# More of the softmax sums on GpSimd, and a new timetable for the side work, in a graph network with masked attention

## The chip, the cores and the metric

The kernel runs on one core of a Trainium2 chip. A core has five engines, each with an instruction stream of its own: TensorE (PE in the profile; PEld is its loading of weights), VectorE (DVE), ScalarE (ACT), GpSimd (POOL) and SyncE (SP), which issues most transfers. The metric is the device time of one execution, in microseconds (us); the time of a kernel is the median of several executions.

## The reference, cut to what matters

The input `x` is 8 batches of 2048 nodes with 256 features; `adj` is a 2048 x 2048 matrix of weights, with zeros. All is in float32. Layer 0 is a graph convolution with two batch norms, layer 1 an attention with 4 heads of 64 over the same nodes, masked where `adj` is 0. Each layer is added to its input, and a layer norm follows.

```python
# layer 0 (inner part cut): agg = A_hat @ x; h = relu(bn(agg @ W1.T)); out = bn(h @ W2.T)
x = _layernorm(x + _L0_gnn_ref(x, adj, ...), axis=-1)

# layer 1
qkv = h @ W                                    # h is the x of the line above
q, k, v = ...                                  # 4 heads of 64
mask = jnp.where(adj == 0, -jnp.inf, 0.0)
scores = jnp.einsum('bhid,bhjd->bhij', q, k) / np.sqrt(HEAD_DIM) + mask
attn = jax.nn.softmax(scores, axis=-1)
out = jnp.einsum('bhij,bhjd->bhid', attn, v)
x = _layernorm(x + out, axis=-1)
```

## The kernel before

The first part (layer 0) is not touched by the change. The attention works in **units**. A unit is one batch `b`, one pair of heads `hp` (2 pairs) and one chunk `c` of 512 query nodes (4 chunks), so a batch has 8 units and the kernel 64. A unit has 16 **steps**, one for each tile of 128 key nodes. In a step TensorE computes the scores of the tile that lies three steps ahead (`scores`), VectorE masks them from PSUM into a tile `prob`, ScalarE takes the exponential in place, and TensorE multiplies the tile of this step with `v` into the PSUM tile `out_ps` (`weigh`). The maximum of a row is not subtracted; the sums are tested at the end, and another path (`attention_with_maxima`) runs if one is out of range.

The divisor of the softmax is a sum over all key nodes. GpSimd adds the `prob` tiles of a unit one onto another (`acc`), and TensorE sums over the partitions by a multiplication with ones. The last tiles of a unit do not go through GpSimd: TensorE takes them directly.

```python
PE_SUM = 3

def add_up(g):
    u, j = divmod(g, NT)                       # NT = 16
    if j == 1:
        accs[u] = ap_.tile([P, 2, CH], F32, name="acc")
        nc.gpsimd.tensor_add(accs[u], probs[g - 1], probs[g])          # L454
    elif 1 < j < NT - PE_SUM:
        nc.gpsimd.tensor_add(accs[u], accs[u], probs[g])               # L456

def finish_out(u):
    ots[u] = ap_.tile([P, CH], F32, name="ot")
    nc.scalar.copy(ots[u], outs[u][:, 0, :])                           # L460
    nc.vector.tensor_add(ots[u], outs.pop(u)[:, 1, :], ots[u])         # L461

def finish_sums(u):
    pm = ps_m.tile([P, BR], F32, name="pm")
    parts = [probs.pop(g) for g in range((u + 1) * NT - PE_SUM, (u + 1) * NT)]
    parts.append(accs.pop(u))
    for n, part in enumerate(parts):
        for h in range(2):
            for q in range(2):
                ... nc.tensor.matmul(pm[r0 : r0 + 32, :], ones[:, :32], part[...], ...)   # L472
    ...
    sts[u] = ap_.tile([P, BR], F32, name="sm")
    nc.scalar.copy(sts[u], pm)                                         # L480

# finish_turn_sums (L486): sums transposed, reciprocals; finish_turn (L499): output transposed;
# finish (L507): output times reciprocal, added to the chunk x1 (VectorE)
```

Beside this the units carry side work: the input of the next batch is made chunk by chunk (load of `y` and `x`; second batch norm `bn` on ScalarE; `norm`: transposes by TensorE, addition and statistics on VectorE; `root`: four small GpSimd instructions, L91, L93, L272, L273, among them a power of -0.5; `apply`: the rescaling on ScalarE, L277; `turn`: transposes back, L332, and a copy, L338; `project`: q, k and v, L363 and L375). A finished chunk gets its last layer norm (`emit_stats`, `root`, `emit`). All small results of TensorE share the PSUM tile name `pm`, which has two buffers; `out_ps` has one, `prob` has 13. A table tells at which step which side task stands:

```python
for u in range(NU - 1):
    b, hp, c = units[u]
    at_step(u + 1, 0, finish_sums, u)
    at_step(u + 1, 3, finish_turn_sums, u)
    at_step(u + 1, 3, finish_turn, u)
    at_step(u + 1, 3, finish, u, 0)
    at_step(u + 1, 4, finish, u, 1)
    if hp == HP - 1:
        j = 6 if c == 2 else 12
        at_step(u + 1, j, inp.emit_stats, b, c)
        at_step(u + 1, j + 2, inp.root, b, c)
        for half in range(2):
            at_step(u + 1, j + 5 + half, inp.emit, b, c, half)
...
# projections stand at steps 6, 9, 12 of a unit; a chunk of the next batch takes two units

with tc.manual_schedule(engines=IN_ORDER):     # TensorE, VectorE, ScalarE, GpSimd: as written
    for g in range(LEAD):                      # LEAD = 3
        mask_scores(g, scores(g))
        exps(g)
    for g in range(NU * NT):
        u, j = divmod(g, NT)
        ahead = g + LEAD < NU * NT
        if ahead:
            st = scores(g + LEAD)              # L415
        if j == NT - 1:
            weigh(g)                           # L445
            finish_out(u)
        if ahead:
            mask_scores(g + LEAD, st)          # L427
            exps(g + LEAD)                     # L433
        for f, args in side.get((u, j), ()):
            f(*args)
        if j < NT - 1:
            weigh(g)
        add_up(g)
```

Of the kernel before, what the change touches and what calls it, by code (L numbers as in the profile page):

```python
# [8 lines left out]
F32 = mybir.dt.float32  # L9
U8 = mybir.dt.uint8  # L10
AF = mybir.ActivationFunctionType
# [15 lines left out]
def tile_gcn_then_masked_attention(  # L27
# [15 lines left out]
    nc = tc.nc  # L43
    PSUM = bass.MemoryType.PSUM
    P = 128
    B, N, D = x.shape
# [3 lines left out]
    NT = N // P  # L50
    ND = D // P
    NH = H // P
    NO = O // P
    CH = 512
    NCH = N // CH
# [226 lines left out]
    class Layer1Input:  # L282
# [4 lines left out]
            self.pool, self.psum, self.x1_bufs = pool, psum, x1_bufs  # L287
            self.x1, self.x1t, self.yt, self.qkv, self.ln = {}, {}, {}, {}, {}

        def load(self, b, c):  # L290
            if c == 0:
                self.x1t[b] = self.pool.tile([P, ND, N], F32, name="x1t", bufs=1)
            y = self.yt[b, c] = self.pool.tile([P, NO, CH], F32, name="yt", bufs=1)
            nc.sync.dma_start(y, y_d[b * NCH + c])
            t = self.x1[b, c] = self.pool.tile([P, TPC, D], F32, name="x1", bufs=self.x1_bufs)
            nc.sync.dma_start(t, rows(b, c, x))

        def bn(self, b, c):
            y = self.yt[b, c]
            for o in range(NO):  # L300
                nc.scalar.activation(
                    y[:, o, :], y[:, o, :], AF.Identity,
                    bias=sh2[:, o : o + 1], scale=sc2[:, o : o + 1],
                )

        def norm(self, b, c, half):
            y = self.yt[b, c]
# [18 lines left out]

        def turn(self, b, c, half):
            t = self.x1[b, c]
            pm = self.psum.tile([P, ND, BR], F32, name="pm")
            for d in range(ND):  # L330
                for i in range(IT):
                    nc.tensor.transpose(  # L332
                        pm[:, d, i * P : (i + 1) * P],
                        t[:, IT * half + i, d * P : (d + 1) * P],
                        ident,
                    )
            r0 = c * CH + half * BR
            nc.scalar.copy(self.x1t[b][:, :, r0 : r0 + BR], pm)  # L338

        def emit_stats(self, b, c):  # L340
            ln = self.ln[b, c] = LayerNorm(self.pool, self.x1[b, c])
            ln.stats(range(TPC))

        def emit(self, b, c, half):
            self.apply(b, c, half)
# [46 lines left out]
    def attention():  # L392


        with tc.tile_pool(name="attn", bufs=2) as ap_, tc.tile_pool(
# [5 lines left out]
            units = [(b, hp, c) for b in range(B) for hp in range(HP) for c in range(NCH)]  # L401
            probs, accs, outs, ots, sts, pms = {}, {}, {}, {}, {}, {}

            PE_SUM = 3

            def scores(g):
                u, j = divmod(g, NT)
# [42 lines left out]
            def add_up(g):  # L450
                u, j = divmod(g, NT)
                if j == 1:
                    accs[u] = ap_.tile([P, 2, CH], F32, name="acc")
                    nc.gpsimd.tensor_add(accs[u], probs[g - 1], probs[g])  # L454
                elif 1 < j < NT - PE_SUM:
                    nc.gpsimd.tensor_add(accs[u], accs[u], probs[g])  # L456

            def finish_out(u):
# [4 lines left out]
            def finish_sums(u):  # L463

                pm = ps_m.tile([P, BR], F32, name="pm")
                parts = [probs.pop(g) for g in range((u + 1) * NT - PE_SUM, (u + 1) * NT)]
                parts.append(accs.pop(u))
                for n, part in enumerate(parts):
                    for h in range(2):
                        for q in range(2):  # L470
                            r0 = 32 * (2 * h + q)
                            nc.tensor.matmul(  # L472
                                pm[r0 : r0 + 32, :], ones[:, :32],
                                part[:, h, q * BR : (q + 1) * BR],
                                start=(n == 0), stop=(n == len(parts) - 1),
                            )
                for g in range(u * NT, (u + 1) * NT - PE_SUM):
                    del probs[g]
                sts[u] = ap_.tile([P, BR], F32, name="sm")
                nc.scalar.copy(sts[u], pm)  # L480
# [30 lines left out]

            LEAD = 3
            side = {}

            def at_step(u, j, f, *args):
                u, j = u + j // NT, j % NT
                side.setdefault((u, j), []).append((f, args))

            per_b = HP * NCH
            for u in range(NU - 1):
                b, hp, c = units[u]
                at_step(u + 1, 0, finish_sums, u)
                at_step(u + 1, 3, finish_turn_sums, u)
                at_step(u + 1, 3, finish_turn, u)
                at_step(u + 1, 3, finish, u, 0)
                at_step(u + 1, 4, finish, u, 1)
                if hp == HP - 1:
                    j = 6 if c == 2 else 12  # L530
                    at_step(u + 1, j, inp.emit_stats, b, c)
                    at_step(u + 1, j + 2, inp.root, b, c)
                    for half in range(2):
                        at_step(u + 1, j + 5 + half, inp.emit, b, c, half)
            for b in range(B):
                u0 = b * per_b
                for c in range(NCH):

                    for n, w in enumerate((1, 2, 0)):
                        at_step(u0 + c, (6, 9, 12)[n], inp.project, b, 1, c, w)  # L540
                    if b + 1 == B:
                        continue

                    late = 3 * (c == NCH - 1)
                    u = u0 + 3 + c
                    at_step(u - 1, 15 + late, inp.load, b + 1, c)
                    at_step(u, 2 + late, inp.bn, b + 1, c)
                    for half in range(2):
                        at_step(u, 6 + 3 * half + late, inp.norm, b + 1, c, half)
                    at_step(u, 11 + late, inp.root, b + 1, c)  # L550
                    for half in range(2):
                        at_step(u, 13 + half + (4 if late else 0), inp.apply, b + 1, c, half)
                    for half in range(2):
                        at_step(u + 1, 4 if late else 1, inp.turn, b + 1, c, half)
                    for n, w in enumerate((1, 2, 0)):
                        at_step(u + 1, (8, 10, 13)[n] if late else (6, 9, 12)[n],
                                inp.project, b + 1, 0, c, w)

            for c in range(NCH):
                inp.load(0, c)  # L560
                inp.bn(0, c)
                for half in range(2):
                    inp.norm(0, c, half)
                inp.root(0, c)
                for half in range(2):
                    inp.apply(0, c, half)
                for half in range(2):
                    inp.turn(0, c, half)
                for w in range(3):
                    inp.project(0, 0, c, w)  # L570

            with tc.manual_schedule(engines=IN_ORDER):
                for g in range(LEAD):
# [10 lines that stand above are left out]
                    if ahead:  # L584
                        mask_scores(g + LEAD, st)
                        exps(g + LEAD)
                    for f, args in side.get((u, j), ()):
                        f(*args)
                    if j < NT - 1:
                        weigh(g)  # L590
                    add_up(g)
                u = NU - 1
                b, _, c = units[u]
                finish_sums(u)
                finish_turn_sums(u)
                finish_turn(u)
                for half in range(2):
                    finish(u, half)
                inp.emit_stats(b, c)
                inp.root(b, c)  # L600
                for half in range(2):
                    inp.emit(b, c, half)

    def attention_with_maxima():

        with tc.tile_pool(name="full", bufs=2) as ap_, tc.tile_pool(
# [8 lines left out]
            inp = Layer1Input(ap_, ps_m, NCH)  # L615
            for b in range(B):
                for c in range(NCH):
                    inp.load(b, c)
                    inp.bn(b, c)
                    for half in range(2):  # L620
                        inp.norm(b, c, half)
                    inp.root(b, c)
                    for half in range(2):
                        inp.apply(b, c, half)
                    for half in range(2):
                        inp.turn(b, c, half)
# [41 lines left out]
                                z, po, sm, z, op0=ALU.mult, op1=ALU.add  # L668
                            )
                for c in range(NCH):  # L670
                    inp.emit_stats(b, c)
                    inp.root(b, c)
                    for half in range(2):
                        inp.emit(b, c, half)
# [66 lines left out]
```

## Time and profile before

| | |
|---|---|
| time, median of 3 | 4022.19 us (4021.13 to 4022.88) |
| profiled execution | span 4024.4 us |
| masking, VectorE, L427 | 1024 times 1219 ns |
| exponential, ScalarE, L433 | 1024 times 1056 ns |
| addition of a `prob` tile, GpSimd, L456 | 704 times 2365 ns |
| sums of `prob` tiles on TensorE, L472 | 96.2 us in all |
| sums of `acc` on TensorE, L472 | 39.4 us in all |

The profile is that of one execution. Busy time is the time in which an engine had at least one instruction in work; shares are of the whole span, in which layer 0 takes the first 1500 us and the attention the rest. In timelines a line gives the start and the duration in us, then engine, source line, operation, the tiles written and read, and how many like instructions were put together ("x8"); a bracket names the idle time before and what ended it. A float32 product appears as two matmul records. TensorE's ends are modelled, so differences between starts are the better measure.

### The profile page before, as it was taken

What the parts mean: (1) busy time and instruction counts of PE and PEld (TensorE: products, weight loads), DVE (VectorE), ACT (ScalarE), POOL (GpSimd) and SP (SyncE); (2) the same over time, 40 slices, a digit from 0 to 9 for tenths busy, and PEclk for the clock granted to TensorE, in tenths of its full rate; (3) what the DMA queues carried; (4) which work ended last, traced back from release to release, by engine and by line L of the source; (5) the groups of instructions that cost most, each with busy time, mean ns of one, the idle gap of its engine ahead of it and who ended that gap; (6) DMA issues with size and microseconds to landing.
All of it is one profiled execution on the core that took longest, in us unless ns stands there. A gap on an engine that the chain in (4) does not pass through costs nothing.

```text
span 4024.4 us, 57339 instructions
## 1 busy us (share of the span) xinstructions
PE 3814.2 (95%) x24226; PEld 1580.8 (39%) x24226; DVE 1938.5 (48%) x2874; ACT 1634.9 (41%) x2005; POOL 1965.4 (49%) x1103
## 2 busy tenths in 40 slices
PE   3599999999997998999999999999999999999997
PEld 3244444444443443333333333333333333333332
DVE  6411111111112443666666666666666666666665
ACT  6000000000001434555555556556555555555554
POOL 0000000000000003778778777777787877877887
PEclk7799999999998998999999999999999999999998
DMA  5110110111003761001001001001001001000000
GB/s 209 65 53 29 45 52 34 50 53 52 32 31 131 233 205 64 5 13 38 12 17 38 12 17 38 12 17 38 12 12 43 12 12 43 12 12 24 10 1 23
DMA packets 77229, 181.80 MB, mean 45 GB/s; under 512 B 6176, under 2 KB 55840, under 8 KB 66592
## 3 DMA queue, kind: packets, MB, share of 16 engines
q1 hardware_dynamic: 67600, 123.49, 9.3%
q0 software_dynamic: 9360, 54.53, 3.3%
q8 instruction: 192, 3.15, 0.3%
q14 instruction: 77, 0.63, 0.1%
HBM read 106.70 MB, written 71.30 MB: 44 GB/s over the span
## 4 chain that ended last, share of the span: by engine, by line
PE 86%; ACT 4%; DVE 3%; issue 1%; POOL 1%; DMA 1%; SPq 0%; ACTq 0%; DVEq 0%; POOLq 0%
PE pa L183 22%; PE out_ps L445 20%; PE st L415 19%; PE pm L363 6%; PE py L229 6%; PE ph L195 5%; PE pm L375 3%; ACT prob L433 2%; ACT x L277 2%; PE pm L472 2%; DVE prob L427 2%; POOL acc L456 1%; PE pm L312 1%; PE pm L499 1%; PE pm L332 1%
## 5 line engine op out<-in xcount | busy, mean ns | idle before, releaser
L456 POOL TENSOR_TENSOR acc<-acc,prob 128x1024 f32<-128x1024 f32 x704 | 1664.9, 2365 | 168.5 <-ACT prob L433 120.6
L427 DVE SCALAR_TENSOR_TENSOR prob<-mask,st 128x1024 f32<-128x1024 uint8 x1024 | 1241.8, 1219 | 648.6 <-PE st L415 640.3
L433 ACT ACTIVATE prob<-prob 128x1024 f32<-128x1024 f32 x1024 | 1080.5, 1056 | 1049.1 <-DVE prob L427 1041.3
L445 PE MATMUL out_ps<-prob,v 64*64 64x512 f32 x8192 | 1089.1, 598 | 0.1
L415 PE MATMUL st<-qt,kt 64*64 64x512 f32 x8192 | 1074.3, 590 | 0.9 <-DVE prob L427 0.9
L183 PE MATMUL pa<-at,xb 128*128 128x512 f32 x2048 | 886.1, 593 | 47.0 <-DMA xb<-in_x_dram 47.0
L183 PEld LDWEIGHTS pa<-at,xb 128*128 128x128 f32 x2048 | 389.8, 190 | 537.7 <-issue 537.7
L204 POOL DMA_DIRECT2D h_d<-h x32 | 17.3, 540 | 1151.3 <-ACT h L202 1151.3
L415 PEld LDWEIGHTS st<-qt,kt 64*64 64x64 f32 x8192 | 313.4, 133 | 567.5 <-issue 505.3
L202 ACT ACTIVATE h<-ph,b1s 128x512 f32<-128x512 f32 x128 | 87.9, 687 | 1066.0 <-PE ph L195 1066.0
L445 PEld LDWEIGHTS out_ps<-prob,v 64*64 64x64 f32 x8192 | 281.6, 132 | 508.7 <-issue 438.7
L190 DVE COPY ag<-pa 128x512 f32<-128x512 f32 x64 | 44.2, 691 | 823.7 <-PE pa L183 823.7
L454 POOL TENSOR_TENSOR acc<-prob 128x1024 f32<-128x1024 f32 x64 | 152.0, 2375 | 284.1 <-ACT prob L433 284.1
L363 PE MATMUL pm<-x1t,wq 128*128 128x512 f32 x512 | 254.8, 622 | 0.9 <-ACT x1t L338 0.9
L229 PE MATMUL py<-hin,w2s 128*128 128x512 f32 x512 | 222.6, 598 | 21.4 <-ACT hin L222 21.4
L195 PE MATMUL ph<-ag,w1s 128*128 128x512 f32 x512 | 231.1, 599 | 0.0
L203 DVE BATCH_NORM_STATS2 st<-h 128x6 f32<-128x512 f32 x128 | 88.9, 694 | 157.1 <-ACT h L202 157.1
L229 PEld LDWEIGHTS py<-hin,w2s 128*128 128x128 f32 x512 | 98.1, 192 | 145.8 <-issue 114.0
L363 PEld LDWEIGHTS pm<-x1t,wq 128*128 128x128 f32 x512 | 88.1, 191 | 160.3 <-issue 150.9
L222 ACT ACTIVATE hin<-hin,sh,sc 128x512 f32<-128x512 f32 x128 | 93.4, 801 | 138.1 <-DMA hin<-h_d 138.1
L195 PEld LDWEIGHTS ph<-ag,w1s 128*128 128x128 f32 x512 | 94.6, 190 | 131.3 <-issue 107.2
L277 ACT ACTIVATE x<-x,ln_nm,ln_rs 128x256 f32<-128x256 f32 x256 | 136.1, 585 | 24.2 <-POOL ln_nm L273 24.2
(83 smaller groups left out, 1815.3 us busy)
## 6 DMA issues: line engine op xcount, KB each, us to landing
h_d<-h POOLq DMA_DIRECT2D x32, 1024.0 KB, 4.1
hin<-h_d SPq DMA_DIRECT2D x32, 1024.0 KB, 5.9
a<-in_adj_dram SPq DMA_DIRECT2D x16, 1024.0 KB, 7.1
xb<-in_x_dram SPq DMA_DIRECT2D x8, 2048.0 KB, 8.1
y_d<-y POOLq DMA_DIRECT2D x32, 512.0 KB, 6.1
yt<-y_d SPq DMA_DIRECT2D x32, 512.0 KB, 3.2
x<-in_x_dram SPq DMA_DIRECT2D x32, 512.0 KB, 3.9
out_dram<-x SPq DMA_DIRECT2D x32, 512.0 KB, 2.9
```

The costliest lines, as they stand in the source:

```text
L183: nc.tensor.matmul(pa, xb[:, m, d * P : (d + 1) * P], at[:, m, c * CH : (c + 1) * CH], start=(m == 0), stop=(m == NT - 1),)
L195: nc.tensor.matmul(ph, w1s[:, d, f * P : (f + 1) * P], ag[:, d, :], start=(d == 0), stop=(d == ND - 1),)
L229: nc.tensor.matmul(py, w2s[:, f, o * P : (o + 1) * P], h[:, f, :], start=(f == 0), stop=(f == NH - 1),)
L277: nc.scalar.activation(self.t[:, i, :], self.t[:, i, :], AF.Identity, bias=self.nm[:, i : i + 1], scale=self.rs[:, i : i + 1],)
L363: nc.tensor.matmul(pm, wq[:, d, wcols], xt[:, d, cols], start=(d == 0), stop=(d == ND - 1))
L375: nc.tensor.matmul(pm[:, j * P : (j + 1) * P], xt[:, d, t * P : (t + 1) * P], wq[:, d, wcols], start=(d == 0), stop=(d == ND - 1),)
L415: nc.tensor.matmul(st[r * HD : (r + 1) * HD, h, :], kt[hs, j * P + r * HD : j * P + (r + 1) * HD], qt[hs, cols], start=True, stop=True,)
L427: nc.vector.scalar_tensor_tensor(p, mask[:, j, cols][:, None, :].to_broadcast([P, 2, CH]), MASKED, st, op0=ALU.mult, op1=ALU.add,)
L433: nc.scalar.activation(probs[g], probs[g], AF.Exp)
L445: nc.tensor.matmul(outs[u][hs, r, :], inp.qkv[b, hp][2][rs, j, hs], probs[g][rs, h, :], start=(j == 0), stop=(j == NT - 1),)
L454: nc.gpsimd.tensor_add(accs[u], probs[g - 1], probs[g])
L456: nc.gpsimd.tensor_add(accs[u], accs[u], probs[g])
```

## The change

The change does three things. It gives GpSimd 15 of the 16 `prob` tiles of a unit (13 before) and TensorE one directly, except in the last three units, where TensorE takes four. It moves the sums of a unit from step 0 of the next unit to step 4, and lets each unit begin with a projection instead (steps 0, 6 and 10). And it draws out the making of a chunk over three units, so that statistics, roots and rescalings stand some steps apart, and the two halves of a transpose are not in the same step. The aim is to take work from TensorE and to have its program wait for no other engine. The rows of the table have numbers with fractions now, which only order the tasks within a step.

```diff
-            PE_SUM = 3
+            def on_pe(u):
+                return 4 if u >= NU - NCH + 1 else 1
...
-                elif 1 < j < NT - PE_SUM:
+                elif 1 < j < NT - on_pe(u):
...
-            for u in range(NU - 1):
+            for u in range(NU):
                 b, hp, c = units[u]
-                at_step(u + 1, 0, finish_sums, u)
-                at_step(u + 1, 3, finish_turn_sums, u)
-                at_step(u + 1, 3, finish_turn, u)
-                at_step(u + 1, 3, finish, u, 0)
-                at_step(u + 1, 4, finish, u, 1)
+                at_step(u + 1, 4, finish_sums, u)
+                at_step(u + 1, 6, finish_turn_sums, u)
+                at_step(u + 1, 6.2, finish_turn, u)
+                at_step(u + 1, 6.2, finish, u, 0)
+                at_step(u + 1, 7, finish, u, 1)
                 if hp == HP - 1:
-                    j = 6 if c == 2 else 12
-                    at_step(u + 1, j, inp.emit_stats, b, c)
-                    at_step(u + 1, j + 2, inp.root, b, c)
                     for half in range(2):
-                        at_step(u + 1, j + 5 + half, inp.emit, b, c, half)
+                        at_step(u + 1, 10.3 + 3 * half, inp.emit_stats, b, c, half)
+                        at_step(u + 2, 3 + half, inp.emit, b, c, half)
+                    at_step(u + 2, 2, inp.root, b, c)
+
+            PROJECT = (0.1, 6.1, 10.1)
+
+            def project_at(u, b, hp, c):
+                for w in range(3):
+                    at_step(u, PROJECT[w], inp.project, b, hp, c, w)
+
             for b in range(B):
                 u0 = b * per_b
+                project_at(u0, b, 0, NCH - 1)
                 for c in range(NCH):
-                    for n, w in enumerate((1, 2, 0)):
-                        at_step(u0 + c, (6, 9, 12)[n], inp.project, b, 1, c, w)
+                    project_at(u0 + 1 + c, b, 1, c)
                     if b + 1 == B:
                         continue
-                    late = 3 * (c == NCH - 1)
                     u = u0 + 3 + c
-                    at_step(u - 1, 15 + late, inp.load, b + 1, c)
-                    at_step(u, 2 + late, inp.bn, b + 1, c)
-                    for half in range(2):
-                        at_step(u, 6 + 3 * half + late, inp.norm, b + 1, c, half)
-                    at_step(u, 11 + late, inp.root, b + 1, c)
+                    at_step(u, 1, inp.load_y, b + 1, c)
+                    at_step(u, 5, inp.load_x, b + 1, c)
+                    for o in range(NO):
+                        at_step(u, 5 + o, inp.bn, b + 1, c, o)
+                    at_step(u, 10, inp.norm, b + 1, c, 0)
+                    at_step(u + 1, 0, inp.norm, b + 1, c, 1)
+                    at_step(u + 1, 4, inp.root, b + 1, c)
                     for half in range(2):
-                        at_step(u, 13 + half + (4 if late else 0), inp.apply, b + 1, c, half)
-                    for half in range(2):
-                        at_step(u + 1, 4 if late else 1, inp.turn, b + 1, c, half)
-                    for n, w in enumerate((1, 2, 0)):
-                        at_step(u + 1, (8, 10, 13)[n] if late else (6, 9, 12)[n],
-                                inp.project, b + 1, 0, c, w)
+                        at_step(u + 1, 7 + half, inp.apply, b + 1, c, half)
+                        at_step(u + 1, 10.2 + 3 * half, inp.turn, b + 1, c, half)
+                    if c < NCH - 1:
+                        project_at(u + 2, b + 1, 0, c)
...
-                for w in range(3):
+                for w in range(3 if c < NCH - 1 else 0):       # ahead of the loop, first batch
                     inp.project(0, 0, c, w)
```

What is left out here splits `load`, `bn` and `emit_stats` into the parts that the table names, and has the last units' side tasks run out after the loop (`for u in (NU, NU + 1)`) in place of a written tail.

More of the change, by code (lines that the diff above doesn't have):

```diff
@@ L288, in __init__, with load_y, load_x, bn @@
             self.x1, self.x1t, self.yt, self.qkv, self.ln = {}, {}, {}, {}, {}
-        def load(self, b, c):
-            if c == 0:
-                self.x1t[b] = self.pool.tile([P, ND, N], F32, name="x1t", bufs=1)
+        def load_y(self, b, c):
             y = self.yt[b, c] = self.pool.tile([P, NO, CH], F32, name="yt", bufs=1)
             nc.sync.dma_start(y, y_d[b * NCH + c])
+        def load_x(self, b, c):
             t = self.x1[b, c] = self.pool.tile([P, TPC, D], F32, name="x1", bufs=self.x1_bufs)
             nc.sync.dma_start(t, rows(b, c, x))
-        def bn(self, b, c):
+        def bn(self, b, c, o):
             y = self.yt[b, c]
[L300 to L304, printed above, removed]
+            nc.scalar.activation(
+                y[:, o, :], y[:, o, :], AF.Identity,
+                bias=sh2[:, o : o + 1], scale=sc2[:, o : o + 1],
+            )
         def norm(self, b, c, half):
@@ L328, in turn @@
             t = self.x1[b, c]
+            if b not in self.x1t:
+                self.x1t[b] = self.pool.tile([P, ND, N], F32, name="x1t", bufs=1)
             pm = self.psum.tile([P, ND, BR], F32, name="pm")
@@ L338, in turn, with emit_stats @@
             nc.scalar.copy(self.x1t[b][:, :, r0 : r0 + BR], pm)
-        def emit_stats(self, b, c):
-            ln = self.ln[b, c] = LayerNorm(self.pool, self.x1[b, c])
-            ln.stats(range(TPC))
+        def emit_stats(self, b, c, half):
+            if half == 0:
+                self.ln[b, c] = LayerNorm(self.pool, self.x1[b, c])
+            self.ln[b, c].stats(range(IT * half, IT * (half + 1)))
         def emit(self, b, c, half):
@@ L465, in finish_sums @@
                 pm = ps_m.tile([P, BR], F32, name="pm")
-                parts = [probs.pop(g) for g in range((u + 1) * NT - PE_SUM, (u + 1) * NT)]
+                parts = [probs.pop(g) for g in range((u + 1) * NT - on_pe(u), (u + 1) * NT)]
                 parts.append(accs.pop(u))
@@ L476, in finish_sums @@
                             )
-                for g in range(u * NT, (u + 1) * NT - PE_SUM):
+                for g in range(u * NT, (u + 1) * NT - on_pe(u)):
                     del probs[g]
@@ L517, in at_step @@
             def at_step(u, j, f, *args):
-                u, j = u + j // NT, j % NT
-                side.setdefault((u, j), []).append((f, args))
+                tasks = side.setdefault((u, int(j)), [])
+                tasks.append((j, f, args))
+                tasks.sort(key=lambda task: task[0])
             per_b = HP * NCH
-            for u in range(NU - 1):
+            for u in range(NU):
                 b, hp, c = units[u]
-                at_step(u + 1, 0, finish_sums, u)
-                at_step(u + 1, 3, finish_turn_sums, u)
-                at_step(u + 1, 3, finish_turn, u)
-                at_step(u + 1, 3, finish, u, 0)
-                at_step(u + 1, 4, finish, u, 1)
+                at_step(u + 1, 4, finish_sums, u)
[3 more added lines that the diff above has]
+                at_step(u + 1, 7, finish, u, 1)
@@ L559, in attention @@
+                    at_step(u, 10, inp.norm, b + 1, c, 0)
+                    at_step(u + 1, 0, inp.norm, b + 1, c, 1)
+                    at_step(u + 1, 4, inp.root, b + 1, c)
+                    for half in range(2):
+                        at_step(u + 1, 7 + half, inp.apply, b + 1, c, half)
+                        at_step(u + 1, 10.2 + 3 * half, inp.turn, b + 1, c, half)
+                    if c < NCH - 1:
+                        project_at(u + 2, b + 1, 0, c)
             for c in range(NCH):
-                inp.load(0, c)
@@ L561, in attention @@
-                inp.bn(0, c)
+                inp.load_y(0, c)
+                inp.load_x(0, c)
+                for o in range(NO):
+                    inp.bn(0, c, o)
                 for half in range(2):
@@ L586, in attention @@
                         exps(g + LEAD)
-                    for f, args in side.get((u, j), ()):
+                    for _, f, args in side.get((u, j), ()):
                         f(*args)
@@ L591, in attention @@
                     add_up(g)
[L592 to L602, printed above, removed]
+                for u in (NU, NU + 1):
+                    for j in range(NT):
+                        for _, f, args in side.get((u, j), ()):
+                            f(*args)
     def attention_with_maxima():
@@ L617, in attention_with_maxima @@
                 for c in range(NCH):
-                    inp.load(b, c)
-                    inp.bn(b, c)
+                    inp.load_y(b, c)
+                    inp.load_x(b, c)
+                    for o in range(NO):
+                        inp.bn(b, c, o)
                     for half in range(2):
@@ L670, in attention_with_maxima @@
                 for c in range(NCH):
-                    inp.emit_stats(b, c)
+                    for half in range(2):
+                        inp.emit_stats(b, c, half)
                     inp.root(b, c)
```

## The prediction

> **What bounds the kernel now.** I read the page's first part, then the busy time in one stretch, then the waits of TensorE there, then the timelines of TensorE and GpSimd over one unit. First the page, busy time by engine:
>
> ```profile
> PE 3814.2 (95%) x24226; PEld 1580.8 (39%) x24226; DVE 1938.5 (48%) x2874; ACT 1634.9 (41%) x2005; POOL 1965.4 (49%) x1103
> ```
>
> GpSimd's 49% hides that it works only in the attention, from about 1550 us on. So take the attention alone. A batch is 8 units of 16 steps, and it repeats every 307.09 us. Busy times in one such stretch (PE, PEld, DVE, ACT, POOL):
>
> ```profile
> 2022.25:2329.34 307.09, 303.00 (x2610) 118.99 (x2609) 199.38 (x296) 173.08 (x209) 240.55 (x129) 1.00 0.07 22
> ```
>
> TensorE is busy 303.00 of 307.09 at clock 1.00, GpSimd 240.55 (78%). What TensorE waits for in the other 4.1 us (us in total, times, longest):
>
> ```profile
> PE pm L332 <- ACT sm L480: 2.4, 3, 0.8
> PE pm L332 <- ACT prob L433: 1.7, 1, 1.7
> ```
>
> Both stand at the turning of a new chunk (L332): three times because the two pm buffers of PSUM are still held by the sums of the unit just ended, once because the rescaling came late. TensorE executes in program order, so **a microsecond taken out of its work is a microsecond of time**, as long as nobody else falls behind. One plain unit on TensorE (start, duration):
>
> ```profile
> 2226.21 1.04 PE L415 MATMUL st<-qt,kt 64*64 64x512 f32 x8
> 2227.18 1.50 PE L472 MATMUL pm<-prob,ones 128*32 128x256 f32 x24
> 2228.49 0.61 PE L472 MATMUL pm<-acc,ones 128*32 128x256 f32 x8
> 2229.04 1.09 PE L445 MATMUL out_ps<-prob,v 64*64 64x512 f32 x8
> 2229.95 1.04 PE L415 MATMUL st<-qt,kt 64*64 64x512 f32 x8
> ...
> 2233.38 1.04 PE L415 MATMUL st<-qt,kt 64*64 64x512 f32 x8
> 2234.35 0.44 PE L486 MATMUL pm<-ident,sm 128*128 128x128 f32 x2
> 2234.62 0.60 PE L499 MATMUL pm<-ident,ot 128*128 128x128 f32 x4
> 2235.16 1.09 PE L445 MATMUL out_ps<-prob,v 64*64 64x512 f32 x8
> 2236.06 1.04 PE L415 MATMUL st<-qt,kt 64*64 64x512 f32 x8
> ```
>
> Read the differences of starts. A bare step (scores and weighing) takes 1.717 us, 16 of them 27.47. The step with the sums takes 2229.95 - 2226.21 = 3.74, so the sums cost 2.02; three tiles of them cost 2228.49 - 2227.18 = 1.31, that is **0.44 us a tile**. The turning of sums and output (L486, L499) costs 2.68 - 1.72 = 0.96. Read in the same way, the three projections of a unit cost 2.07, 2.14 and 2.08. Together 36.74; the next unit's sums start 36.75 us later. The same unit on GpSimd, then a root:
>
> ```profile
> 2226.34 2.37 POOL L454 TENSOR_TENSOR acc<-prob 128x1024 f32<-128x1024 f32 x1 [3.06 <-ACT prob L433]
> 2230.12 26.80 POOL L456 TENSOR_TENSOR acc<-acc,prob 128x1024 f32<-128x1024 f32 x11 [1.41 <-ACT prob L433]
> 2263.09 2.37 POOL L454 TENSOR_TENSOR acc<-prob 128x1024 f32<-128x1024 f32 x1 [6.17 <-ACT prob L433]
> ...
> 2325.61 0.23 POOL L91 TENSOR_SCALAR ln_rs<-ln_mv 128x4 f32<-128x4 f32 x1
> ```
>
> An add comes every 26.80 / 11 = 2.436 us. The second add starts 3.78 us after the first, held by its tile. 6.17 us are free at the unit's end. The four instructions of a root run from 2325.61 to the next add at 2327.50: 1.89 us.
>
> **What the Trainium skill says.** "GPSIMD Engine Reference", section "Elementwise — side-by-side cycle accounting", gives 4497 ns for a two-input fp32 add of 2048 elements; half of it is an estimate of 2250 ns for our 1024. The trace has 2365 ns; I use the trace. The same page, "Specifications", says that GpSimd's SBUF interface is shared with VectorE and collides with VectorE instructions that have two SBUF inputs or run in a two-port mode. Our masking reads one input from PSUM, and the 572 adds of the middle batches take 2351/2365/2391 ns (min, median, max) beside a VectorE 65% busy: no collision shows. "TensorEngine Tiling (Array Packing)", "Key Properties", says that a change of tiling mode drains TensorE. The trace agrees: scores (64x64) to sums takes 0.97 instead of 0.86, weighing to scores after it 0.91, so each side group costs some 0.15 beyond its matmuls. "Perfetto Trace Analysis", "Optimization Strategy", says that the same gap repeating on the engine that should be saturated can mean too few buffers: the 0.8 us at L332, three times a batch, is that.
>
> **The change part by part.**
>
> *Sums.* For units 0 to 60 TensorE sums one tile and the accumulator, not three tiles and the accumulator: 2 x 0.44 = 0.88 us a unit less. Units 61 to 63 sum four tiles, 0.44 more each.
>
> *GpSimd.* Two more adds a unit, 14. A plain unit is 3.78 + 13 x 2.436 = 35.45 us from the first add to the end of the last. A root inside the run (step 4, in four units of a batch) adds 1.89; a root at step 2 lies between the first and the second add, where 1.41 us are idle anyway, and adds 0.5. Over a batch: 8 x 35.45 + 4 x 1.89 + 4 x 0.5 = 293.2.
>
> *Sums at step 4, a projection at step 0.* The projection (2.07) takes the place of the sums (2.02) as what TensorE does while ScalarE and VectorE empty the output PSUM (585 and 691 ns, L460, L461), so no wait opens there. The sums move four steps (about 9 us) later, so GpSimd's accumulator is not waited for even if it is a few us late.
>
> *Merged groups.* The turning goes into the step of the second projection: one side group less, about 0.1 us saved. Norm transposes were beside a projection and stay so; one turning of the new chunk is now beside a projection and the other stands alone, about the same sum as the pair before.
>
> *The 4.1 us.* The halves of the turning are now three steps apart, and the roots 2 to 4 steps ahead of the rescaling. Where three pm tiles follow one another in one step (steps 6 and 10), a projection of 2 us lies between the first and the third, longer than the copy that frees the first (VectorE: up to 1.22 of masking, then 0.17 or 0.69). I expect these waits gone.
>
> A plain unit is then 36.75 - 0.88 - 0.10 = 35.77 on TensorE; a batch 303.0 - 8 x 0.98 = **295.2**, against 293.2 on GpSimd. TensorE stays the bound, narrowly.
>
> *Start.* The last chunk's first projections (three, 5.4 us) leave the stretch ahead of the loop for unit 0, which gives its own to unit 1. Unit 0's weighing now waits until chunk 3 is turned (before: at 1579.7), then needs 0.9 + 15 x 1.72 + 2.07 + 2.14 + 1.9 = 32.8: unit 1 at 1612.5, against 1612.0 before. But steps of unit 0 no longer stand between the transposes of chunks 1 to 3, where they delayed the chain by 1 to 3 us each. I choose 1608.
>
> *Units 1 to 55.* 7 x 295.2 - 35.8 = 2030.6: unit 56 at 3638.6 (before 3725.3).
>
> *Last batch.* Five units with projections, 5 x 35.77 = 178.9; unit 61 without: 27.5 + 1.15 + 0.96 = 29.6; two with four tiles: 30.9 each; and these three have nothing at step 0 to cover the emptying of the output, about 0.85 us each, 2.6. Sum 272.9: 3911.5.
>
> *Tail.* Before, the last weighing ended at 3992.2 and the program at 4024.4, 32.2 us, with this wait in it:
>
> ```profile
> PE pm L472 <- POOL acc L456: 4.3, 1, 4.3
> ```
>
> The last units were paced by GpSimd (12 adds and a root, 31.1 us). With 11 adds (26.8) it is ahead, the wait goes, a tile of 0.44 comes: 28.4. End at 3939.9 in the profile's span. The profiled span is 2.2 us over the median of the times: **3938 us**.
>
> **The rivals.** (1) *GpSimd becomes the bound.* Its batch is 293 of 295. If adds took 0.1 us more when back to back, 13 x 8 x 0.1 = 10 us a batch, it would pace the kernel at 303, and the end would be near 3995. For it: the thin margin. Against: the adds already run eleven back to back at 2.436. (2) *A new PSUM wait takes the old one's place:* three pm tiles in one step, four to twelve times a batch. At 0.5 us each that is 2 to 6 us a batch, 3952 to 3980. For it: the waits of 0.8 now are of this kind. Against: the projection in between. (3) *A rescaling waits for a root behind a busy GpSimd,* ScalarE's exponentials wait behind it, then TensorE. For it: the 1.7 us now; against: at least one step, mostly three, between them. About 1 us a batch, 3945. (4) *The sums were hidden anyway, so nothing is gained.* 303.00 busy of 307.09 speaks against it.
>
> **Range and chances.** The start is uncertain by 4 us, the tail by 3, a leftover wait of 0 to 2 us a batch adds up to 14; below, merged groups could give 0.1 us a unit more. I take 3926 to 3960. Two per cent is at 3941.7, just above my value: faster by over 2% 0.55, within 2% 0.43, slower 0.02.
>
> **What would show it.** Batch period 295 us, TensorE busy at least 99% of it; the sums of probability tiles about 37 us instead of 96 in all; adds still 2.37 us, GpSimd some 290 us a batch; no waits at L332. It is wrong if waits at L332, L499 or L472 fill more than 2 us a batch, or if the adds grow.

## The result, and the profile after

The changed kernel takes 3921.4 us (3918.9 to 3922.8), against 4022.5 for the kernel before: a ratio of 0.9746, 95% interval 0.9729 to 0.9763. The gain of 101 us is larger than predicted (84), and the time lies 4.6 us below the stated range.

The page's first part, busy time by engine:

```profile
PE 3732.8 (95%) x23274; PEld 1553.8 (40%) x23274; DVE 1935.4 (49%) x2874; ACT 1641.3 (42%) x2005; POOL 2245.5 (57%) x1222
```

TensorE has 81 us less to do, GpSimd 280 us more, VectorE and ScalarE the same. A batch repeats every 292.13 us, 14.96 less than before. Busy times in one batch (PE, PEld, DVE, ACT, POOL, then clock and transfers):

```profile
2009.88:2302.01 292.13, 292.13 (x2488) 115.59 (x2484) 198.88 (x296) 173.94 (x208) 278.18 (x144) 1.00 0.07 23
```

TensorE is never idle in it. The 4.1 us of waits a batch are gone. In the whole attention after unit 0, up to the final test of the sums, the list of TensorE's waits has two entries, both in the last units (us in total, times, longest):

```profile
PE out_ps L449 <- DVE ot L465: 1.7, 3, 0.6
PE pm L490 <- ACT sm L484: 1.6, 1, 1.6
```

The timeline of TensorE over one unit shows where its work went (start, duration):

```profile
1982.77 1.04 PE L419 MATMUL st<-qt,kt 64*64 64x512 f32 x8
1983.74 0.64 PE L476 MATMUL pm<-prob,ones 128*32 128x256 f32 x8
1984.19 0.61 PE L476 MATMUL pm<-acc,ones 128*32 128x256 f32 x8
1984.74 1.09 PE L449 MATMUL out_ps<-prob,v 64*64 64x512 f32 x8
1985.65 1.04 PE L419 MATMUL st<-qt,kt 64*64 64x512 f32 x8
...
1987.36 1.04 PE L419 MATMUL st<-qt,kt 64*64 64x512 f32 x8
1988.33 0.44 PE L490 MATMUL pm<-ident,sm 128*128 128x128 f32 x2
1988.61 1.88 PE L365 MATMUL pm<-x1t,wq 128*128 128x512 f32 x4
1990.33 0.60 PE L503 MATMUL pm<-ident,ot 128*128 128x128 f32 x4
1990.86 1.09 PE L449 MATMUL out_ps<-prob,v 64*64 64x512 f32 x8
1991.77 1.04 PE L419 MATMUL st<-qt,kt 64*64 64x512 f32 x8
```

From scores to scores the step with the sums takes 2.88 us: 1.16 for the sums, where it was 2.02. The step in which the turning stands around a projection takes 1991.77 - 1987.36 = 4.41, so the group costs 2.69. Apart, before, the same matmuls cost 0.96 + 2.07 = 3.03. **Standing together saves 0.34 us**, and no instruction was dropped. Where it lies shows beside the projection that stands alone at step 0 of the same unit:

```profile
1974.79 1.98 PE L365 MATMUL pm<-x1t,wq 128*128 128x512 f32 x4
1976.71 1.09 PE L449 MATMUL out_ps<-prob,v 64*64 64x512 f32 x8
```

Start to start, the four products take 1.92 us up to the weighing, but 1.72 up to the transposes at step 6: 0.20 lies inside this block, and only about 0.15 at the edges of the group (0.97 and 0.91 where a bare step has 0.86). The new chunk's second turning, which stands alone, shows the same from the other side:

```profile
2078.85 1.04 PE L419 MATMUL st<-qt,kt 64*64 64x512 f32 x8
2079.82 0.66 PE L333 MATMUL pm<-ident,x 128*128 128x128 f32 x4
2080.41 1.09 PE L449 MATMUL out_ps<-prob,v 64*64 64x512 f32 x8
2081.32 1.04 PE L419 MATMUL st<-qt,kt 64*64 64x512 f32 x8
```

2.47 - 1.72 = 0.75 us for four transposes alone. The same four beside a projection add 0.43 (that step goes from 4.26 to 4.69).

GpSimd is now nearly full, too. Its waits in the same batch:

```profile
POOL acc L460 <- ACT prob L437: 3.5, 3, 1.4
POOL acc L458 <- ACT prob L437: 0.4, 1, 0.4
```

It waits only 3.9 us of 292.1; the other idle time, some 10 us, lies between its own instructions (an add takes 2.37 us, as before, and one starts every 2.436). VectorE now waits for GpSimd to free a `prob` tile, 6.0 us a batch; TensorE does not.

### The profile page after: what moved, and what is told of

It is laid out like the page before. It is cut to its first block, busy times and chain, and to the rows that moved or that the text cites. A ratio compares the mean times of both kernels' runs of the same rounds, so it can differ in the third digit from the quotient of the medians.

```text
span 3918.3 us, 55545 instructions
## 1 busy us (share of the span) xinstructions
PE 3732.8 (95%) x23274; PEld 1553.8 (40%) x23274; DVE 1935.4 (49%) x2874; ACT 1641.3 (42%) x2005; POOL 2245.5 (57%) x1222
## 4 chain that ended last, share of the span: by engine, by line
PE 93%; DVE 1%; POOL 1%; DMA 1%; ACT 1%; issue 0%; SPq 0%; POOLq 0%; DVEq 0%; ACTq 0%
PE out_ps L449 23%; PE pa L183 23%; PE st L419 22%; PE pm L365 6%; PE py L229 6%; PE ph L195 6%; PE pm L377 3%; PE pm L476 2%; PE pm L311 1%; PE pm L333 1%; PE pm L503 1%; PE pm L490 1%; DVE at L168 1%; POOL acc L460 1%; DMA hin<-h_d 0%; ACT x L277 0%
## 5 line engine op out<-in xcount | busy, mean ns | idle before, releaser
L460 POOL TENSOR_TENSOR acc<-acc,prob 128x1024 f32<-128x1024 f32 x823 | 1948.5, 2368 | 101.7 <-ACT prob L437 43.9
L449 PE MATMUL out_ps<-prob,v 64*64 64x512 f32 x8192 | 1077.0, 596 | 1.7 <-DVE ot L465 1.7
L229 PE MATMUL py<-hin,w2s 128*128 128x512 f32 x512 | 222.9, 598 | 21.6 <-ACT hin L222 21.6
L238 POOL DMA_DIRECT2D y_d<-y x32 | 17.1, 533 | 224.2 <-DVE y L236 224.2
```

The lines of the kernel that those rows point to most:

```text
L229: nc.tensor.matmul(py, w2s[:, f, o * P : (o + 1) * P], h[:, f, :], start=(f == 0), stop=(f == NH - 1),)
L449: nc.tensor.matmul(outs[u][hs, r, :], inp.qkv[b, hp][2][rs, j, hs], probs[g][rs, h, :], start=(j == 0), stop=(j == NT - 1),)
```

## The experiments

The theory (A): TensorE is the bound and runs in program order, so each microsecond of its work or its waits is one of time; the gain is tiles, waits and merged groups. The rivals: GpSimd paces the changed kernel (C); the sums were hidden and the timetable did it all (B); and about the size of a merged group, my own 0.10 us. Times are medians of four or more runs.

**The timetable alone.**

```diff
 def on_pe(u):
-    return 4 if u >= NU - NCH + 1 else 1
+    return 3
```

> The changed kernel with three prob tiles summed by TensorE in every unit, as before: the new timetable alone. Theory A (TensorE is the bound, and its work decides): 61 units get 2 tiles back at 0.44 us, three units lose one, +52.4 us against the changed kernel's 3921, so about 3974 (3970 to 3979); batch period 292.1 + 7.0 = 299.2 us, TensorE busy all of it, GpSimd at some 240 us a batch. So the timetable is worth about 48 us of the 101 and the tiles 53. Rival B (the sums were hidden and the timetable brought everything): about 3921. Rival C (GpSimd paces the changed kernel, so giving it less work brings something back): less than +40 us.

Measured: 3974.0 us, ratio to before 0.9882 (0.9866 to 0.9899). The batch is 299.03 us, TensorE busy all of it, GpSimd 240.28. With the new timetable in place two tiles a unit are worth 52.6 us; the timetable itself is worth 48.3. B and C fall: giving GpSimd less to do brought nothing back.

**The tiles alone**, in the kernel before:

```diff
-PE_SUM = 3
+PE_SUM = 1
```

> The kernel before with 15 prob tiles added on GpSimd in every unit (PE_SUM = 1), sums still at step 0: the tiles alone. Theory A: 0.88 us a unit less on TensorE, and the accumulator is ready just in time in most units (35.4 us of adds from step 0, sums at some 37 us), while the last four units, which have no projections, are paced by GpSimd at 36 us instead of 31: 4022 - 53 + 20 + a few us of waits for the accumulator, about 3992 (3980 to 4005). Rival (without the move to step 4 TensorE waits for the accumulator in every unit, 1 to 2 us): 4030 to 4090, and waits of the sums for GpSimd of 60 us or more. Rival (hidden sums): 4022 or more.

Measured: 4013.1 us, 0.9976 (0.9969 to 0.9983), slower than expected: without the new timetable only 9 of the 53 us arrive. What TensorE waits for the accumulator, in one batch of the middle and then in the last units:

```profile
PE pm L472 <- POOL acc L456: 0.5, 1, 0.5
PE pm L472 <- POOL acc L456: 20.2, 4, 7.2
```

The rival with a wait for the accumulator in every unit is wrong: in the middle the waits for it are 0.5 us a batch. The last units, paced by GpSimd as expected, wait 20.2 us: this is what the special case of four tiles is for. The batch is 303.04 us, 4.05 less than before where the tiles give 7.04. A plain unit shows nearly the full 0.88 (36.75 to 35.89). What is missing lies in four of the eight units. In three of them, which turn a new chunk at step 1, the step with the sums takes 3.63 us and not 2.88, and the next one 4.04 and not 3.92; in the fourth the step with the sums takes 3.20. That is 2.9 of the 3.0 us. In two of the four `out_ps` waits for VectorE (0.9 us a batch, first seen here): the shortened sums at step 0 no longer cover the emptying of the output there. In the other two the accumulator is late. So the projection at the head of a unit helps once the sums are short, though not in every unit.

**One side group more.**

```diff
-at_step(u + 1, 6, finish_turn_sums, u)
-at_step(u + 1, 6.2, finish_turn, u)
-at_step(u + 1, 6.2, finish, u, 0)
-at_step(u + 1, 7, finish, u, 1)
+at_step(u + 1, 8, finish_turn_sums, u)
+at_step(u + 1, 8.2, finish_turn, u)
+at_step(u + 1, 8.2, finish, u, 0)
+at_step(u + 1, 9, finish, u, 1)
```

> The changed kernel with the turning of sums and output at step 8 (its product at 8 and 9), alone, not around the projection at step 6: one side group more in each unit, no instruction more. Theory A (entering and leaving a side group costs TensorE about 0.34 us, so merging two groups was worth 0.34 us a unit; the trace of the changed kernel has 2.69 us for the merged step, 0.96 + 2.07 apart): 61 x 0.34 = +21 us, about 3942 (3937 to 3946). The prediction's own figure of 0.10 us a group: 3927. Rival C (GpSimd paces the units, TensorE has slack): 3921 to 3924.

Measured: 3948.1 us, 0.9815 (0.9798 to 0.9831): 26.7 us more with the same instructions. In its timeline the projection alone costs 2.07 and the turning alone 0.96 again. That is the 0.34 a unit, 21 us; the other 5 to 6 lie in step 10 of the units with norm transposes, 0.21 us longer. There the projection follows the norm transposes after 0.63 us and not 0.49; I take it that its pm buffer comes free later, since VectorE's product of the turned output now ends only 0.15 us before. The profile lists no wait there, so this is argued and not shown. The prediction's 0.10 us is wrong.

**The order within a group.**

```diff
-at_step(u + 1, 6.2, finish_turn, u)
+at_step(u + 1, 6.05, finish_turn, u)     # ahead of the projection at 6.1
```

> The changed kernel with the turning of the output ahead of the projection of step 6 instead of after it: the same work, but the third pm tile of the step, the projection's, is asked for right after the second, and must wait until VectorE has copied the sums out of the first, behind its masking. Theory A (the projection between hides that wait): a wait of 0.6 to 0.8 us in each of the 61 units with a projection, 3958 to 3970. Rival (two pm buffers are enough whatever the order, the waits before had another cause): 3921 within 4 us.

Measured: 3980.4 us, 0.9891 (0.9874 to 0.9907), 59 us more, beyond the 37 to 49 expected. The whole run's waits of TensorE have a new entry:

```profile
PE pm L365 <- DVE sums_all L492: 41.3, 60, 0.7
```

60 waits of 0.69 us: the third pm tile of the step waits for VectorE to empty the first. That is the wait the projection hides in the changed kernel, and of the kind that stood at L332 before. The step costs 0.95 us more than in the changed kernel; the 0.26 beyond the listed wait I take for the pipeline that runs empty in it, which no run isolates. The run with the tiles alone shows as much: a listed wait of 0.46 us for `out_ps` made its step 0.75 longer.

**A second merging, at another tile shape.** The sums stand right behind the projection of step 0, in the units where no norm transposes are there:

```diff
-at_step(u + 1, 4, finish_sums, u)
+beside = (u + 1) % per_b < NCH or u + 1 > NU - NCH + 1
+at_step(u + 1, 0.2 if beside else 4, finish_sums, u)
```

> The changed kernel with the sums of a unit at step 0 of the next, right after the projection there, wherever no norm transposes stand at that step (units 0 to 3 of a batch, 31 units), and at step 0 in units 62, 63 and after the last: one side group less in each, no instruction more or less. Theory A (a side group costs some 0.34 us to enter and leave): 31 x 0.34 = 10.5 us less, and 2 to 3 us at the end, where the sums now cover the emptying of the output: 3908 (3905 to 3912). Rival (what costs is each change of tile shape, and the sums have a shape of their own, so half of it stays): 31 x 0.17 + 3, about 3913. Rival (GpSimd's accumulator, ready some 0.3 to 2.2 us into the unit, is not ready when the sums come, 2.9 us into it): waits of the sums for GpSimd, 3921 or more.

Measured: 3914.7 us, 0.973 (0.9714 to 0.9747); no wait for GpSimd. The gain of 6.7 us is the rival's size, not the 13 of A. The timeline:

```profile
1974.31 1.04 PE L419 MATMUL st<-qt,kt 64*64 64x512 f32 x8
1975.28 1.98 PE L365 MATMUL pm<-x1t,wq 128*128 128x512 f32 x4
1977.19 0.64 PE L476 MATMUL pm<-prob,ones 128*32 128x256 f32 x8
1977.65 0.61 PE L476 MATMUL pm<-acc,ones 128*32 128x256 f32 x8
1978.20 1.09 PE L449 MATMUL out_ps<-prob,v 64*64 64x512 f32 x8
1979.11 1.04 PE L419 MATMUL st<-qt,kt 64*64 64x512 f32 x8
```

4.80 - 1.72 = 3.08 us against 2.07 + 1.16 apart: 0.15 saved. Read the shapes. Apart, TensorE goes 64x64, 128x128, 64x64, 128x32, 64x64: four changes; here three. Turning and projection have the same shape, and merging them took four changes to two, for 0.34. So theory A is corrected: **what costs is each change of tile shape, 0.15 to 0.17 us on average**, not a group as such.

**All 16 tiles on GpSimd.**

```diff
-    return 4 if u >= NU - NCH + 1 else 1
+    return 4 if u >= NU - NCH + 1 else 0
```

> The changed kernel with all 16 prob tiles of units 0 to 60 added on GpSimd, TensorE summing the accumulator alone there. Theory A, with GpSimd only just below TensorE at 15 tiles: 15 adds x 2.436 x 8 = 292.3 us and 8 roots x 1.89 = 15.1 us make at least 307.4 us a batch on GpSimd, against 292.1 - 3.5 on TensorE, so GpSimd becomes the bound: 3921 + 7.6 x 15.3 = 4037 (4025 to 4060), GpSimd busy nearly all of a batch, TensorE waiting for it at the sums or for prob buffers. Rival (13 prob buffers and the sums at step 4 take up what GpSimd is late): TensorE has 0.44 us a unit less, 3894.

Measured: 4026.0 us, 1.0007 (1.0 to 1.0014). The timeline of GpSimd, first adds of two units a batch apart:

```profile
2030.30 2.37 POOL L458 TENSOR_TENSOR acc<-prob 128x1024 f32<-128x1024 f32 x1
2337.67 2.38 POOL L458 TENSOR_TENSOR acc<-prob 128x1024 f32<-128x1024 f32 x1
```

307.37 us, the 307.4 of its adds and roots, and no idle time in front of either. TensorE waits 13.5 us a batch, 4.8 for the accumulator and 8.7, where the sums are turned, for ScalarE's copy of them. One tile more undoes the whole change: at 15 tiles the two engines are within 1.3% of each other (3.9 us of waits in 292.1).

**Both turnings beside other work.** On top of the kernel with merged sums:

```diff
-at_step(u + 1, 7 + half, inp.apply, b + 1, c, half)
-at_step(u + 1, 10.2 + 3 * half, inp.turn, b + 1, c, half)
+at_step(u + 1, 5 + half, inp.apply, b + 1, c, half)
+at_step(u + 1, (6.3, 10.2)[half], inp.turn, b + 1, c, half)
```

> As e5_sums_beside_q, and the new chunk's rescaling two steps earlier (steps 5 and 6), its turning beside other work: the first half at the end of the group at step 6, the second in the group at step 10, none alone at step 13. Theory A: another 28 groups x 0.32 us = 9 us less where no pm buffer is missing, about 3900; but the first half is the fourth pm tile in its step and comes 0.5 us after the projection's end, before VectorE has copied that away (0.15 + 0.69 us): a wait of some 0.3 us takes most of it back, so 3900 to 3909 against e5's 3908. Rival (ScalarE is overloaded at steps 5 and 6: exponential, rescaling and second norm, 3.0 us in a step of 1.7): waits for ScalarE, above 3912.

Measured: 3937.6 us, 0.9786 (0.977 to 0.9803), 23 us worse, by something that nobody expected. ScalarE's waits in one batch:

```profile
ACT x1t L339 <- PE pm L377: 9.5, 1, 9.5
```

`x1t` has one buffer. The first chunk of the next batch now wants to write it at step 6 of a unit in which the old batch's last projection (L377) reads it at step 10. ScalarE stops for 9.5 us, and on TensorE that unit takes 40.7 us. In the other units the first half waits 0.4 us for its pm buffer, and a unit takes 37.8 us; in the changed kernel both kinds take 37.5.

**The start.** On top of the kernel with merged sums, chunk 3's q, which unit 0 does not need, goes from step 0 to step 12:

```diff
-at_step(u, PROJECT[w], inp.project, b, hp, c, w)
+at_step(u, 12.1 if u == w == 0 else PROJECT[w], inp.project, b, hp, c, w)
```

> e5_sums_beside_q with one projection moved: chunk 3's q in unit 0 from step 0 to step 12 (it is not needed before unit 3), so that unit 0's first steps no longer wait for chunk 3. In the changed kernel TensorE ran the stretch 1572 to 1580 us at a granted clock of 0.50, with gaps of 5 us, and unit 1 began 102.7 us after the batch norm's factors were ready (before: 102.1), so the shorter program ahead of the loop brought nothing. Theory (unit 0's steps, kept back, were what filled those gaps and kept the clock up): unit 0 runs to step 6 beside the making of chunks 1 to 3 and needs some 24 us after it instead of 33: unit 1 some 8 us earlier, clock above 0.75 there, 3915 - 8 = 3907 (3904 to 3910). Rival (the chain of the chunks sets the start, whatever fills it, and steps among its transposes delay it as much as they gain): 3912 to 3917.

Measured: 3907.6 us (3903.7 to 3908.5), 0.9716 (0.97 to 0.9732): 7.1 us less than the kernel it starts from, as the theory said. From the batch norm's factors to unit 1 it takes 95.6 us in the profiled execution (104.4 in the kernel it starts from, 102.7 in the changed kernel, 102.1 before). Busy times around the end of the start, two stretches of the changed kernel and then one of this (PE first, the clock third from the end):

```profile
1572.00:1576.00 4.00, 2.62 (x9) 1.66 (x10) 0.00 (x0) 3.25 (x6) 0.01 (x1) 0.50 0.00 0
1576.00:1580.00 4.00, 4.00 (x8) 1.23 (x12) 0.00 (x0) 0.43 (x1) 0.00 (x0) 0.50 0.00 0
1572.00:1580.00 8.00, 8.00 (x52) 2.74 (x51) 2.92 (x3) 4.41 (x6) 3.81 (x2) 0.83 0.01 2
```

With nothing to do between the chunks TensorE went at half clock; with unit 0's steps there it works all the time at 0.83. How much of the gain is the clock and how much the steps done earlier, the run does not separate. This is the fastest version tried, 13.8 us below the changed kernel.

## Why the prediction was right or wrong

- **The bound: right.** TensorE is busy all of a batch, GpSimd close below; the first shows in the busy times after, the second in the run with 16 tiles.
- **Sums: right.** 0.88 us a unit was worked out and 0.86 measured (2.02 to 1.16); over all units 52.4 us follow from it, and the run with the timetable alone gives 52.6. L476 for probability tiles is at 44.8 us in all, not 37: a group of 24 matmul records is busy for 1.50 us, but one of 8 for 0.64, more than a third of that. It is a figure of busy time and cost nothing.
- **Waits at L332: right,** 4.1 us a batch gone, none new. The run with the timetable alone has none either, so the table removed them; its parts were not run one by one. That the projection between keeps a new wait away, as argued, is shown by the order experiment.
- **GpSimd: right about who paces, too high in its load.** Adds take 2.37 us, and TensorE never waits for the accumulator. But the 293.2 us worked out for GpSimd are more than the 292.1 that a batch takes: the sum counted as work the 1.41 us for which the second add of a unit waits. Adds (14 for 15 tiles) and roots alone are 8 x 14 x 2.436 + 8 x 1.89 = 288.0. Rivals 1, 2 and 3 did not come; 4 is refuted.
- **Merged groups: the step that failed.** "One side group less, about 0.1 us saved" measures 0.34 a unit, and "about the same sum as the pair before" measures 0.28 less a chunk (1.97 for norm and turning transposes against 2.25). A batch: 8 x 0.24 + 4 x 0.28 = 3.0 us, nearly the whole difference between 295.2 and 292.1; units 1 to 55 took 2009.4 us, not 2030.6, which is 21.2 less. I had read 0.97 and 0.91 in place of 0.86 at the edges of a group and took the 0.15 for all that a group costs. But another 0.20 lay inside what I had booked as matmuls (1.92 against 1.72 above). The trace before also holds it: the turning, six transposes alone, costs 0.96 there, and four transposes beside a projection 0.39 to 0.44, which makes some 0.6 for six.
- **Start: wrong by 2.6 us the other way.** Unit 1 began at 1610.6, not 1608. Some luck hides in this: the batch norm's factors, which the change does not touch, were ready 2.1 us earlier in this execution. From the factors, the projection that follows the turning of chunk 3 began after 67.9 us (before: 69.7): sooner, as argued, but by 1.9 us and not by the 4.5 that 1608 asks for. From there unit 0 took 34.9 us, not 32.8: at half clock its first projection and weighing took 2.1 us more.
- **Last batch and tail:** units 56 to 63 took 269.9 us to the last weighing, not 272.9, and the tail 28.4, as worked out.
- **Sum:** +2.6 - 21.2 - 3.0 = -21.6 us in the span. The predicted time lay 2.2 us below its span, the measured median 3.1 above; this 5.3 goes the other way, by chance. Together, with rounding, 16.6 us: 3938 to 3921.4. The range allowed for less than what one step got wrong.

## What to carry to other kernels

On an engine that works in order, price side work by where it stands, not only by what it is: measure the same instructions alone and beside others of the same tile shape, start to start over the whole step. Three tiles from a two-buffer pool in one step need something long between the first and the third. When work goes to a helper engine, compute its load per period to the last instruction: of 13, 15 and 16 tiles (14 was not tried) 15 were the best, and 16 gave all back.

## What the runs showed of the hardware that I had not expected

A change of TensorE's tile shape costs 0.15 to 0.17 us on average in float32, worked out from 0.34 us for two changes fewer and 0.15 for one fewer. "TensorEngine Tiling (Array Packing)", "Key Properties", in the Trainium skill says that such a change drains the engine; it gives no cost, and these are the numbers. They agree with a drain, but no run separates it from the loading of the next weights.

Thinning out a stretch can slow what stays. In the start of the changed kernel TensorE had gaps of 5 us and was granted a clock of 0.50, and four projection records took 3.78 us there, against 1.98 at full clock. "TensorE: Matmul & The Clock Gate", section "What's actually happening", says that the gate falls to half after an idle window of about 3.4 us; the gaps of 5 us and the 0.50 agree. But shorter gaps did it too: in the last version TensorE was idle for 2.44 us up to 1570.87, and from 1571.3 to 1574.6 its clock was 0.50.
